# Paired values, fp4 multiplications of three chunks on GpSimd and new due times in a planned two-layer kernel

## The chip, the cores and the metric

The kernel runs on one core of one Trainium2 chip. The metric is the device time of one execution in microseconds (us). The core has five engines that run their own instruction streams: TensorE (PE, with its weight loads as PEld), VectorE (DVE), ScalarE (ACT), GpSimd (POOL) and SyncE (SP), which here issues every DMA. All of the kernel's data are float32 at the interface.

## The reference

The input is `x` of shape [8, 1024, 256]: 8 sequences of 1024 rows. Four residual steps follow one another, each on a layernorm of `x` without gain:

```
x = x + L0_attn(layernorm(x))   # decoder layer with causal "flow" attention, 16 heads of 16, wo, layernorm,
                                # gelu FFN 256 -> 1024 -> 256, layernorm
x = x + L0_ffn(layernorm(x))    # relu(n @ w1 + b1) @ w2 + b2, width 1024
x = x + L1_attn(layernorm(x))   # softmax attention over 1024 rows, one head of 256
x = x + L1_ffn(layernorm(x))    # fp4(silu(fp4(n) @ fp4(wg).T) * (fp4(n) @ fp4(wu).T)) @ fp4(wd).T, width 704
```

The second attention is what the change's first part touches:

```
Q, K, V = split(t @ W_qkv.T + b_qkv);  softmax(Q @ K.T / sqrt(256)) @ V
```

`fp4` takes blocks of 16 neighbours of a row, scales each by its largest magnitude over 6, rounds to the grid 0, 0.5, 1, 1.5, 2, 3, 4, 6 and scales back. It is applied to the weights and to both inputs of the last FFN's matmuls, so that the gated product `hid` (128 rows by 704) of every chunk passes through it.

## The kernel before

**Tiling.** The 8192 rows are 64 chunks of 128 (`P`). Four chunks (`G`) make a group, 16 groups in all, two to a sequence, eight chunks (`NCH`) to a sequence. Matmuls take 128 by 128 weights and stream 128 to 512 columns into one of eight PSUM banks. The first layer runs group by group: flow attention on 32-row tiles of TensorE (the rows of the profile with `kz`), the two dense FFNs as two loops over eight blocks of the width (`w_in` into `hidden`, `hidden` into `w_out`), then `norms_1` and `norms_2`. The dense weights don't stay in SBUF: `load_weights` streams them for each group, 256 KB a load, into two buffers of `w_in` and two of `w_out`, so that a load can start only when the matmuls on the buffer's last content are done. The second layer runs chunk by chunk in `soft_chunk`, once all eight chunks of a sequence have been normed: scores against both groups of keys, exponentials, transposed probabilities times the values `vt`, then fp4 of the normed rows, gate and up, `hid`, fp4 of `hid`, down, and the output.

**norms_2** ends the first layer for a chunk: layernorm `n`, the turn of `n` into `n2T` (256 features on partitions, rows in the free dimension; it serves as key, query input and value input), and then two matmuls with `wv3` for the chunk's values, and one DVE addition of the bias row `bsv` into `vt`. `q["normed"]` counts the chunks of a sequence that are through.

**fp4** on a `hid` of 128x704: a maximum per block of 16 (`x_amax`), the scale `x_s` and its reciprocal `x_r` (128x44 each), a multiplication by the reciprocal and a constant (`hid<-hid,x_r`), a square on ACT into `q_c`, two DVE steps that round by adding and subtracting, and a multiplication by the scale (`hid<-hid,x_s`). The turn of `hid` into `hqT` follows.

**flip** turns a 128x256 block in one of two ways. The far way is a copy on POOL into `cut` (as 16-bit halves), a DMA transpose on SP's queue into `spun` and a copy on ACT. The near way is two transposes on PE into a bank and a copy on ACT. The near way is taken where the planner finds that PE is short of ready work (`plan.idle`).

**The order** of all instructions on every engine is made when the program is built. Each part of the work is a generator that yields what its next instruction needs; `Plan` holds a clock for each engine, costs every instruction in `took`, and always advances the part that could start with the least wait for PE, ties going to the part with the earliest due time `at`. The engines then run exactly in that order: each instruction has a dependence on the one before it on its engine. Due times and waits come from the table `T`, overridden by the entries of `EARLY`, each of which holds until a time on the planner's PE clock (130, 260, 400, 2150 and the end). Where the planner expects PE to stand still for over 1.6 us, `fill` puts dummy multiplications of the identity by itself there (`bank<-ident` in the profile). `Queue.issue` records every instruction, so that all rows of the profile carry its line, L431, and are told apart by tile names: `mx` is the row maximum of the scores, `prob` the exponentials, `ln_ve` and `ln_rstd` the two steps of a layernorm on POOL, `res` and `xr` residual rows with a bias added on POOL.

Of the kernel before, what the change touches and what calls it, by code (L numbers as in the profile page):

```python
# [14 lines left out]
ALU = mybir.AluOpType  # L15
AX = mybir.AxisListType

P = 128
D = 256
# [4 lines left out]
INTER = 704  # L24
# [7 lines left out]
    span=-0.073, prods=0.129, pair=0.137, sums=0.037, weighted=0.239, sums2=0.231, chunk=0.625,  # L32
# [5 lines left out]
    gate1=1, gate2=1, by_act=1,  # L38
)
LAG = 2  # L40
QB = 16
G = 4
GT = G * P
# [41 lines left out]
        gate2=3.5,  # L85
# [6 lines left out]
        gate1=3.5, prods=0.091, weights=0.002,  # L92
    )),
    (400.0, dict(
        prods=-0.044, pair=0.237, weighted=0.037, chunk=0.696, turn_k=0.968, xo=0.327,
        turn_h=0.707, step=0.103, norm=0.746, soft=3.784, soft1=0.31, soft3=0.912, fp4=2.195,
        weights=0.078, ripe_d=7.107, ahead=0.839, lin2=-0.414, dense1=-0.101, norm1=0.415,
    )),
    (2150.0, dict(
        span=-0.281, prods=-0.047, pair=0.211, sums=0.062, weighted=0.312, scores=0.625,  # L100
        turn_k=0.801, xo=0.501, turn_h=0.706, soft3=1.013, fp4=3.733, fp4_over=6.383,
        ripe_g=0.463, ripe_d=6.945, back=1.258, ahead=1.548, lin1=0.497, lin2=-0.186,
        lin3=-0.398, dense0=0.006, dense1=-0.298, norm0=-0.113, norm1=-0.214, weights0=-0.286,
        gate1=3, shy=0.438, gate2=4, lin0=0.25,
    )),
    (1000000000.0, dict(
        lin3=0.54, ripe_d=5.647, lin1=0.423, dense1=-0.149, scores=0.713, ripe_g=0.601, xo=0.287,
        chunk=0.609, shy=1.216, back=0.633, sums2=0.358, ripe_t=0.0, soft2=0.39, ahead=1.438,
        step=0.155, span=-0.165, weights=0.092, ripe_s=0.0, fp4=3.709, turn_k=0.743,
        weighted=0.307, norm=0.386, fp4_over=3.982, sums=-0.024, gate1=2, prods=0.13, gate2=3.5,  # L110
        norm1=0.603, lin0=0.38,
    )),
]

# [18 lines left out]
class Plan:  # L133
# [96 lines left out]
    def took(self, queue, op, args, kw):  # L230

        aps = [x for x in list(args) + list(kw.values()) if isinstance(x, bass.AP)]
        outs = [kw["out"] if "out" in kw else aps[0]]
        if kw.get("accum_out") is not None:
            outs.append(kw["accum_out"])
        size = 1
        for ap in aps:
            n = 1
            for d in ap.shape[1:]:
                n *= d  # L240
            size = max(size, n)

        overlap, after = 0.0, 0.035
        if queue == "tensor":
            size = 1
            for d in outs[0].shape[1:]:
                size *= d
            cost = size * (0.853e-3 if op == "transpose" else 1.687e-3)
            tiled = op == "matmul" and (kw["lhsT"].shape[-1] <= 32 or kw["lhsT"].shape[0] <= 32)
            if tiled or op == "matmul" and kw["lhsT"].dtype == BF16:  # L250
                cost *= 0.25
            if tiled != self.tiled:
                cost += 0.2
            self.tiled = tiled
            after = 0.2
        elif queue == "vector":
            each = {"reciprocal": 6.2e-3, "tensor_tensor_scan": 2.15e-3}.get(op, 1.05e-3)
            cost = 0.17 + each * size
            if op == "tensor_scalar" and outs[0].dtype == BF16:
                cost = 0.16 + 0.26e-3 * size  # L260
            elif op == "scalar_tensor_tensor" and any(ap.shape[-1] == 1 for ap in aps):
                cost += 0.06
            if size >= 256 and not any(ap.tensor.name in self.banks for ap in aps):
                cost *= 1.12
            overlap = 0.08
        elif queue == "scalar":
            cost = (0.16 if op == "copy" and outs[0].dtype != U16 else 0.26) + 0.82e-3 * size
            for x in args:
                if not isinstance(x, bass.AP) and self.SETS.get(x, self.act_set) != self.act_set:
                    self.act_set = self.SETS[x]  # L270
                    self.free[queue] = self.free.get(queue, 0.0) + 1.3
            if kw.get("accum_out") is not None:
                cost += 0.15
            overlap = 0.1
        elif queue == "gpsimd":
            cost = 0.65 + 0.7e-3 * size
            if op in ("tensor_scalar", "iota"):
                cost = 0.22
            elif op == "memset":
                cost = 0.1 + 0.9e-3 * size  # L280
            elif op == "tensor_copy":
                cost = 0.2 + 1.0e-3 * size
        else:
            wide = op != "dma_start_transpose" and size > 256
            cost = 1.34 if op == "dma_start_transpose" else 0.6 if wide else 0.54
        start = self.free.get(queue, 0.0)
        if queue not in ("tensor", "sync"):
            start = max([start] + [self.used.get(ap.tensor.name, 0.0) for ap in outs])
        for ap in aps:
            name = ap.tensor.name  # L290
            if self.by.get(name) != queue or queue in ("vector", "gpsimd"):
                start = max(start, self.done.get(name, 0.0) + (0.05 if queue == "gpsimd" else 0.0))
            if name not in self.done and name in self.held:
                start = max(start, self.used[name])
        if queue == "tensor":
            if start - self.ran > 2.0:
                self.slow = start + 2.1
            if start < self.slow:
                cost *= 2
            self.ran = start + cost  # L300
        if queue == "sync":
            start = max(start, self.landed.pop(0))
        end = start + cost
        if queue == "sync":
            n = 2e-6 / 180e-3 if op == "dma_start_transpose" else 4e-6 / 320e-3
            for d in outs[0].shape:
                n *= d
            self.free["rings"] = max(self.free.get("rings", 0.0), end) + n
            after = self.free["rings"] - end + (0.75 if op == "dma_start_transpose" else 1.8)
            self.landed.append(end + after)  # L310
        self.free[queue] = end - overlap
        for ap in outs:
            self.done[ap.tensor.name] = end + after
            self.by[ap.tensor.name] = queue
        for ap in aps:
            name = ap.tensor.name
            self.used[name] = max(self.used.get(name, 0.0), end + after)
            if queue != "tensor" and name not in self.kept:
                self.held.discard(name)
# [17 lines left out]
    def pe(self, *tiles, **kw):  # L337
        return self.need("tensor", tiles, **kw)
# [111 lines left out]
def block_stack_kernel(ctx: ExitStack, tc: tile.TileContext, a: dict, out: bass.AP):  # L450
# [346 lines left out]
    def two(t):  # L797
        return t.rearrange("p (k t) -> p k t", k=2)

    def blocks(t, width):  # L800
        return t[:, :width].rearrange("p (b e) -> p b e", e=QB)

    def wide(v, rows, nb):
        return v.unsqueeze(2).to_broadcast([rows, nb, QB])

    def fp4(src, width, rows=P, factor=1.0):

# [13 lines left out]
        rc = small([P, INTER // QB], "x_r", 2)[:rows, :nb]  # L823
        nc.vector.reciprocal(rc, sc)
        yield dve(rc)
        nc.vector.scalar_tensor_tensor(
            blocks(src, width),
            blocks(src, width),
            -factor * (1.0 - 2.0**-23),
            wide(rc, rows, nb),  # L830
            ALU.mult,
            ALU.mult,
        )
        tile_c = yield from fresh("q_c", act(src))
        c = tile_c[:rows, :width]
        nc.scalar.activation(c, src, AF.Square, scale=(2.0**22 / 6.0) ** 0.5)
# [3 lines left out]
        yield dve(src)  # L840
        nc.vector.scalar_tensor_tensor(src, c, k, src, ALU.add, ALU.subtract)
        plan.drop(tile_c)
        nc.vector.tensor_tensor(
            blocks(src, width), blocks(src, width), wide(sc, rows, nb), ALU.mult
        )

# [156 lines left out]
    def running(out, cur, carry, b, first, last):  # L1003
# [14 lines left out]
    flows = B * NG  # L1018
    seqs = [{"past": {"chunks": 0}, "n2T": {}, "vt": {}, "normed": 0} for _ in range(B)]
    groups = [  # L1020
        {"res": {}, "hT": {}, "nT": {}, "turned": {}, "scaled": set(), "ran": set(), "away": {}}
        for _ in range(flows)
    ]
    count = {
# [669 lines left out]
    def norms_2(p, i, acc, taken):  # L1694
# [14 lines left out]
        if g not in q["n2T"]:  # L1709
            q["n2T"][g] = two(kept([P, 2 * GT], "n2T", 4))  # L1710
        n2 = q["n2T"][g]
        here = slice(i * P, (i + 1) * P)
        yield from flip(two(n), n2[:, :, here], last=n)
        yield pe(
            n2,
            banks=1,
            when=lambda: "values" in late
            and (s < 2 or count["valued"] >= (s - 1) * NCH)
            and (p == 0 or count["attended"] >= 3 * G),
        )  # L1720
        if g not in q["vt"]:
            q["vt"][g] = kept([P, G, D], "vt", 4)
        bank = mm_bank()
        for k in range(2):
            nc.tensor.matmul(
                bank[:, :D], lhsT=n2[:, k, here], rhs=wv3[:, k, :], start=k == 0, stop=k == 1
            )
        yield dve(bank)
        nc.vector.tensor_tensor(q["vt"][g][:, i, :], bank[:, :D], bsv, ALU.add)
        q["normed"] += 1  # L1730


    def soft_chunk(cc):
# [120 lines left out]
            nc.vector.tensor_tensor(hid[:, cols], hid[:, cols], ub, ALU.mult)  # L1854
        plan.drop(xqT)
        yield dve(hid)
        yield from fp4(hid, INTER, factor=0.5)
        hqT, pairs = [], []
        for half in range(2):
            tq = yield from fresh("prob", plan.pool(hid, at=at + times["soft3"]), "hqT")  # L1860
# [91 lines left out]
```

## Time and profile before

| what | value |
|---|---|
| runs | 2435.72, 2436.44, 2437.16 us; median 2436.44 |
| the profiled execution's own time | 2438.24 us |
| its span (first to last instruction) | 2436.5 us |
| its mean granted clock | 0.998 |
| busy: PE, DVE, ACT, POOL | 2411.5, 1899.1, 1408.5, 1255.0 us |
| last PE instruction ends at | 2433.2 us |
| DMA: share of 16 engines by SP's transfers, transposes issued | 53.0%, 771 |
| ACT table loads | 139, 1.283 us each |

In a row of a group of instructions stand line, engine, operation, output<-inputs, shapes, count, then busy time and the mean ns of one, then the engine's idle time just ahead of them with what ended it. In the timeline a row begins with its start and length in us, and a bracket tells a wait ahead of it and its releaser; `x8` counts instructions that were drawn together. A busy PE is one that has a matmul in its pipeline.

### The profile page before, as it was taken

The page shows a single profiled execution, that of the slowest core. Times are in us where ns is not written, and L with a number is a line of the kernel's source. Part 1 is how long each engine was busy: PE and PEld are TensorE (multiplying, and loading weights), DVE is VectorE, ACT ScalarE, POOL GpSimd, SP SyncE. Part 2 cuts the span into 40 slices and gives each one's busy share as a digit, 9 for nine tenths or more (in the row PEclk, how much of TensorE's full clock was granted, in tenths as well). Part 3 has the DMA queues.
Part 4 walks back from the last instruction along what each step waited for, and adds up shares of the span by engine and source line. Part 5 has one row for each costly group of instructions (what it writes and reads, how often), then busy time and mean ns, then how long its engine had stood idle before and what let it go on. Part 6 is the DMA issues. An engine that isn't in the chain of part 4 may idle for free.

```text
span 2436.5 us, 46855 instructions
## 1 busy us (share of the span) xinstructions
PE 2411.5 (99%) x16103; PEld 1868.0 (77%) x16103; DVE 1899.1 (78%) x4121; ACT 1408.5 (58%) x2882; POOL 1255.0 (52%) x2261
## 2 busy tenths in 40 slices
PE   8999999999999999999999999999999999999998
PEld 6787777777777777787777777787777777787766
DVE  7887776878778787787869778787877968766688
ACT  5546455465565645656565565655656665545454
POOL 4455364453655655456454655556464664534342
PEclk9999999999999999999999999999999999999999
DMA  4354665455655554556555555555555655645333
GB/s 105 106 168 140 171 139 149 117 118 130 141 130 132 136 146 116 141 132 141 135 124 136 142 132 128 127 146 118 150 128 120 158 110 138 139 112 133 67 76 70
DMA packets 633103, 313.62 MB, mean 129 GB/s; under 512 B 436000, under 2 KB 621344, under 8 KB 632864
## 3 DMA queue, kind: packets, MB, share of 16 engines
q1 hardware_dynamic: 632864, 310.62, 53.0%
q8 instruction: 128, 2.10, 0.4%
q14 instruction: 111, 0.91, 0.1%
HBM read 188.43 MB, written 20.97 MB: 86 GB/s over the span
## 4 chain that ended last, share of the span: by engine, by line
PE 91%; DVE 5%; ACT 2%; POOL 1%; DMA 1%; issue 1%; DVEq 0%; POOLq 0%; ACTq 0%; SPq 0%
PE bank L431 91%; DVE prod L431 1%; DVE hid L431 1%; ACT L431 1%; POOL ln_rstd L431 0%; DVE u L431 0%; DVE ln_st L431 0%; DVE x_amax L431 0%; DMA w_in<-in_L_attn_W_dram 0%; DVE k L431 0%; POOL ln_ve L431 0%; POOL ln_shift L431 0%; ACT kz L431 0%; DVE q L431 0%; DVE sc L431 0%
## 5 line engine op out<-in xcount | busy, mean ns | idle before, releaser
L431 PE MATMUL bank<-half,w_in 128*128 128x256 f32 x2048 | 530.0, 382 | 2.5 <-DMA w_in<-in_L_attn_W_dram 1.4
L431 PE MATMUL bank<-w_out,hidden 128*128 128x256 f32 x2048 | 527.7, 384 | 3.6 <-DMA w_out<-in_L_attn_W_dram 2.6
L431 PEld LDWEIGHTS bank<-w_out,hidden 128*128 128x128 f32 x2048 | 380.2, 190 | 105.3 <-issue 46.1
L431 PEld LDWEIGHTS bank<-half,w_in 128*128 128x128 f32 x2048 | 384.1, 190 | 79.9 <-issue 20.0
L431 POOL TENSOR_SCALAR ln_ve<-ln_mv 128x1 f32<-128x1 f32 x384 | 99.8, 260 | 559.3 <-DVE ln_mv L431 528.5
L431 ACT ACTIVATE hidden<-bank,c_L_ffn_b 128x256 f32<-128x256 f32 x256 | 120.7, 472 | 222.9 <-PE bank L431 222.0
L431 POOL TENSOR_TENSOR ln_rstd<-ln_ve,neghalf 128x1 f32<-128x1 f32 x384 | 232.8, 606 | 32.0
L431 PE MATMUL bank<-n2T,qT 128*128 128x512 f32 x512 | 241.6, 594 | 0.0
L431 ACT ACTIVATE hidden<-bank,c_L_attn_b 128x256 f32<-128x256 f32 x256 | 119.7, 469 | 196.4 <-PE bank L431 195.1
L431 PE MATMUL bank<-vt,probT 128*128 128x256 f32 x1024 | 233.0, 381 | 0.0
L431 POOL COPY cut<-n 128x512 uint16<-128x512 uint16 x231 | 166.4, 726 | 110.5 <-DVE n L431 73.4
L431 PEld LDWEIGHTS bank<-vt,probT 128*128 128x128 f32 x1024 | 195.2, 191 | 33.2 <-issue 4.8
L431 POOL COPY cut<-prob 128x512 uint16<-128x512 uint16 x229 | 161.4, 727 | 86.4 <-ACT prob L431 57.2
L431 POOL COPY cut<-hid 128x512 uint16<-128x512 uint16 x170 | 120.2, 730 | 133.3 <-DVE rsum L431 50.5
L431 ACT ACT_TABLE_LOAD x139 | 178.3, 1283 | 6.8 <-DVE nmax L431 3.2
L431 PE MATMUL bank<-wdT,hqT 128*128 128x256 f32 x768 | 176.4, 379 | 0.1
L431 PE MATMUL bank<-wgT,xqT 128*128 128x352 f32 x512 | 172.8, 460 | 0.8 <-ACT xqT L431 0.8
L431 PE MATMUL bank<-wuT,xqT 128*128 128x352 f32 x512 | 172.4, 459 | 0.0
L431 ACT COPY probT<-spun 128x512 uint16<-128x512 uint16 x251 | 161.2, 672 | 16.0 <-DMA spun<-cut 15.4
L431 PEld LDWEIGHTS bank<-wdT,hqT 128*128 128x128 f32 x768 | 145.4, 190 | 22.9 <-issue 1.4
L431 PEld LDWEIGHTS bank<-n2T,qT 128*128 128x128 f32 x512 | 96.2, 190 | 69.5 <-issue 60.3
L431 DVE TENSOR_TENSOR sc<-bank,tri 128x384 f32<-128x384 f32 x240 | 116.7, 546 | 39.1 <-PE bank L431 39.0
(294 smaller groups left out, 4741.7 us busy)
## 6 DMA issues: line engine op xcount, KB each, us to landing
w_in<-in_L_attn_W_dram SPq DMA_DIRECT2D x128, 256.0 KB
w_out<-in_L_attn_W_dram SPq DMA_DIRECT2D x128, 256.0 KB
w_in<-in_L_ffn_w_dram SPq DMA_DIRECT2D x128, 256.0 KB
w_out<-in_L_ffn_w_dram SPq DMA_DIRECT2D x128, 256.0 KB
spread<-packed SPq DMA_DIRECT2D x90, 256.0 KB
spun<-cut SPq DMA_TRANSPOSE x771
x<-in_L_attn_inputs_dram SPq DMA_DIRECT2D x64, 128.0 KB
xr<-in_L_attn_inputs_dram SPq DMA_DIRECT2D x64, 128.0 KB
```

The costliest lines, as they stand in the source:

```text
L431: ins = method(*args, **kw)
```

## The change

Three things. In `norms_2` the values of chunks 2j and 2j+1 of a group are made together when both are turned: four matmuls into the halves of one bank, and one DVE addition of 128x512 with the bias row broadcast. In `fp4` of `hid`, for chunks 59, 60 and 61 (`POOLED`), the multiplication by the reciprocal and that by the scale go to GpSimd; the constant is then multiplied into the 128x44 reciprocal on DVE first. The planner costs such a GpSimd instruction at 1.5 us. And three of the five entries of `EARLY` have new values: those until 400, until 2150 and to the end.

```diff
@@ -38,6 +38,7 @@
     gate1=1, gate2=1, by_act=1,
 )
 LAG = 2
+POOLED = (59, 62)
 QB = 16
 G = 4
 GT = G * P
@@ -92,23 +93,24 @@
         gate1=3.5, prods=0.091, weights=0.002,
     )),
     (400.0, dict(
-        prods=-0.044, pair=0.237, weighted=0.037, chunk=0.696, turn_k=0.968, xo=0.327,
-        turn_h=0.707, step=0.103, norm=0.746, soft=3.784, soft1=0.31, soft3=0.912, fp4=2.195,
-        weights=0.078, ripe_d=7.107, ahead=0.839, lin2=-0.414, dense1=-0.101, norm1=0.415,
+        prods=-0.044, pair=0.237, weighted=0.037, chunk=0.696, turn_k=0.968, xo=0.316,
+        turn_h=0.707, step=0.103, dense=-0.082, norm=0.746, soft=3.784, soft1=0.31, soft3=0.912,
+        fp4=2.195, weights=0.264, shy=0.202, ripe_t=1.123, ripe_d=7.107, ahead=0.839,
+        lin2=-0.414, dense1=-0.101, norm1=0.415, soft2=0.206,
     )),
     (2150.0, dict(
-        span=-0.281, prods=-0.047, pair=0.211, sums=0.062, weighted=0.312, scores=0.625,
-        turn_k=0.801, xo=0.501, turn_h=0.706, soft3=1.013, fp4=3.733, fp4_over=6.383,
-        ripe_g=0.463, ripe_d=6.945, back=1.258, ahead=1.548, lin1=0.497, lin2=-0.186,
-        lin3=-0.398, dense0=0.006, dense1=-0.298, norm0=-0.113, norm1=-0.214, weights0=-0.286,
-        gate1=3, shy=0.438, gate2=4, lin0=0.25,
+        span=-0.205, prods=-0.047, pair=0.211, sums=0.062, weighted=0.312, turn_k=0.801,
+        xo=0.501, turn_h=0.706, soft3=1.013, fp4=3.733, fp4_over=7.303, ripe_g=0.463,
+        ripe_d=6.945, back=1.258, ahead=1.548, lin1=0.397, lin2=-0.186, lin3=-0.398,
+        dense0=0.006, dense1=-0.8, norm0=-0.113, norm1=-0.214, weights0=-0.286, weights1=-0.074,
+        gate1=3, shy=0.438, gate2=4, lin0=0.25, weights=0.303,
     )),
     (1000000000.0, dict(
-        lin3=0.54, ripe_d=5.647, lin1=0.423, dense1=-0.149, scores=0.713, ripe_g=0.601, xo=0.287,
-        chunk=0.609, shy=1.216, back=0.633, sums2=0.358, ripe_t=0.0, soft2=0.39, ahead=1.438,
-        step=0.155, span=-0.165, weights=0.092, ripe_s=0.0, fp4=3.709, turn_k=0.743,
-        weighted=0.307, norm=0.386, fp4_over=3.982, sums=-0.024, gate1=2, prods=0.13, gate2=3.5,
-        norm1=0.603, lin0=0.38,
+        ripe_d=4.893, lin1=0.423, dense1=0.15, scores=0.713, ripe_g=0.601, xo=0.287, chunk=0.609,
+        shy=1.216, back=0.503, sums2=0.358, ripe_t=0.0, soft2=0.39, ahead=1.438, step=0.155,
+        span=-0.165, weights=0.053, ripe_s=0.0, fp4=3.709, turn_k=0.743, weighted=0.307,
+        norm=0.387, fp4_over=3.982, sums=0.005, gate1=2, prods=0.13, gate2=3.5, norm1=0.328,
+        lin0=0.38, soft1=0.406, pair=0.17, ripe_v=0.561, weights0=-0.456, lin=0.147,
     )),
 ]
 
@@ -280,6 +282,8 @@
                 cost = 0.1 + 0.9e-3 * size
             elif op == "tensor_copy":
                 cost = 0.2 + 1.0e-3 * size
+            elif size > 512:
+                cost = 1.5
         else:
             wide = op != "dma_start_transpose" and size > 256
             cost = 1.34 if op == "dma_start_transpose" else 0.6 if wide else 0.54
@@ -803,7 +807,7 @@
     def wide(v, rows, nb):
         return v.unsqueeze(2).to_broadcast([rows, nb, QB])
 
-    def fp4(src, width, rows=P, factor=1.0):
+    def fp4(src, width, rows=P, factor=1.0, pooled=False):
 
@@ -823,14 +827,21 @@
         rc = small([P, INTER // QB], "x_r", 2)[:rows, :nb]
         nc.vector.reciprocal(rc, sc)
         yield dve(rc)
-        nc.vector.scalar_tensor_tensor(
-            blocks(src, width),
-            blocks(src, width),
-            -factor * (1.0 - 2.0**-23),
-            wide(rc, rows, nb),
-            ALU.mult,
-            ALU.mult,
-        )
+        if pooled:
+            nc.vector.tensor_scalar(rc, rc, -factor * (1.0 - 2.0**-23), None, ALU.mult)
+            yield plan.pool(rc)
+            nc.gpsimd.tensor_tensor(
+                blocks(src, width), blocks(src, width), wide(rc, rows, nb), ALU.mult
+            )
+        else:
+            nc.vector.scalar_tensor_tensor(
+                blocks(src, width),
+                blocks(src, width),
+                -factor * (1.0 - 2.0**-23),
+                wide(rc, rows, nb),
+                ALU.mult,
+                ALU.mult,
+            )
         tile_c = yield from fresh("q_c", act(src))
         c = tile_c[:rows, :width]
         nc.scalar.activation(c, src, AF.Square, scale=(2.0**22 / 6.0) ** 0.5)
@@ -840,7 +851,9 @@
         yield dve(src)
         nc.vector.scalar_tensor_tensor(src, c, k, src, ALU.add, ALU.subtract)
         plan.drop(tile_c)
-        nc.vector.tensor_tensor(
+        if pooled:
+            yield plan.pool(src)
+        (nc.gpsimd if pooled else nc.vector).tensor_tensor(
             blocks(src, width), blocks(src, width), wide(sc, rows, nb), ALU.mult
         )
 
@@ -1018,7 +1031,7 @@
     flows = B * NG
     seqs = [{"past": {"chunks": 0}, "n2T": {}, "vt": {}, "normed": 0} for _ in range(B)]
     groups = [
-        {"res": {}, "hT": {}, "nT": {}, "turned": {}, "scaled": set(), "ran": set(), "away": {}}
+        {"res": {}, "hT": {}, "nT": {}, "turned": {}, "scaled": set(), "ran": set(), "away": {}, "there": set()}
         for _ in range(flows)
     ]
     count = {
@@ -1711,23 +1724,38 @@
         n2 = q["n2T"][g]
         here = slice(i * P, (i + 1) * P)
         yield from flip(two(n), n2[:, :, here], last=n)
+        there = groups[p]["there"]
+        there.add(i)
+        if i % 2 == 0:
+            return
         yield pe(
             n2,
             banks=1,
-            when=lambda: "values" in late
+            when=lambda: i - 1 in there
+            and "values" in late
             and (s < 2 or count["valued"] >= (s - 1) * NCH)
             and (p == 0 or count["attended"] >= 3 * G),
         )
         if g not in q["vt"]:
             q["vt"][g] = kept([P, G, D], "vt", 4)
         bank = mm_bank()
-        for k in range(2):
-            nc.tensor.matmul(
-                bank[:, :D], lhsT=n2[:, k, here], rhs=wv3[:, k, :], start=k == 0, stop=k == 1
-            )
+        for j in range(2):
+            for k in range(2):
+                nc.tensor.matmul(
+                    bank[:, j * D : (j + 1) * D],
+                    lhsT=n2[:, k, (i - 1 + j) * P : (i + j) * P],
+                    rhs=wv3[:, k, :],
+                    start=k == 0,
+                    stop=k == 1,
+                )
         yield dve(bank)
-        nc.vector.tensor_tensor(q["vt"][g][:, i, :], bank[:, :D], bsv, ALU.add)
-        q["normed"] += 1
+        nc.vector.tensor_tensor(
+            q["vt"][g][:, i - 1 : i + 1, :],
+            bank.rearrange("p (j d) -> p j d", d=D),
+            bsv.unsqueeze(1).to_broadcast([P, 2, D]),
+            ALU.add,
+        )
+        q["normed"] += 2
 
     def soft_chunk(cc):
@@ -1854,7 +1882,7 @@
             nc.vector.tensor_tensor(hid[:, cols], hid[:, cols], ub, ALU.mult)
         plan.drop(xqT)
         yield dve(hid)
-        yield from fp4(hid, INTER, factor=0.5)
+        yield from fp4(hid, INTER, factor=0.5, pooled=POOLED[0] <= cc < POOLED[1])
         hqT, pairs = [], []
         for half in range(2):
             tq = yield from fresh("prob", plan.pool(hid, at=at + times["soft3"]), "hqT")
```

## The prediction

> **What bounds the kernel now.** First the page: span, busy shares, chain.
>
> ```profile
> span 2436.5 us, 46855 instructions
> ...
> PE 2411.5 (99%) x16103; PEld 1868.0 (77%) x16103; DVE 1899.1 (78%) x4121; ACT 1408.5 (58%) x2882; POOL 1255.0 (52%) x2261
> ...
> PE 91%; DVE 5%; ACT 2%; POOL 1%; DMA 1%; issue 1%; DVEq 0%; POOLq 0%; ACTq 0%; SPq 0%
> ```
>
> TensorE is busy for 2411.5 of 2436.5 us, so at most 25.0 us of waits can be won without taking matmuls away. Next, stretches of 60 us tell where they lie (columns: stretch; us, busy PE, PEld, DVE, ACT, POOL with counts; granted clock, DMA share, GB/s).
>
> ```profile
> 240.00:300.00 60.00, 57.44 (x465) 47.75 (x464) 49.80 (x116) 27.25 (x67) 23.88 (x47) 1.00 0.62 168
> 360.00:420.00 60.00, 57.80 (x310) 44.90 (x308) 37.63 (x85) 38.29 (x75) 28.41 (x51) 1.00 0.62 149
> 420.00:480.00 60.00, 59.59 (x365) 45.92 (x366) 49.57 (x105) 28.98 (x64) 23.32 (x42) 0.97 0.50 126
> 480.00:540.00 60.00, 58.71 (x461) 45.23 (x460) 40.47 (x100) 37.14 (x75) 37.91 (x74) 0.97 0.50 115
> 1740.00:1800.00 60.00, 60.00 (x307) 47.03 (x307) 50.16 (x104) 30.48 (x64) 29.16 (x52) 1.00 0.60 144
> ```
>
> Between 540 and 2340 us the stretches look like the last one: nothing to win. The waits are before 540 and in the tail, and two stretches also show a clock of 0.97, which is 60 x 0.03 = 1.8 us each. The timeline shows the two waits ahead of these dips.
>
> ```profile
> 414.55 1.97 SPq L431 DMA_TRANSPOSE spun<-cut  x1
> 416.61 0.54 SPq L431 DMA_DIRECT2D w_out<-in_L_attn_W_dram  x1
> 417.26 1.78 SPq L431 DMA_TRANSPOSE spun<-cut  x1
> 420.41 3.36 PE L431 MATMUL bank<-w_out,hidden 128*128 128x256 f32 x8 [2.62 <-DMA w_out<-in_L_attn_W_dram]
> ...
> 503.51 1.34 PE L431 MATMUL bank<-q,kz 32*128 32x128 f32 x32 [1.29 <-ACT kz L431]
> ```
>
> The load of w_out stood in SP's queue behind a transpose, was issued at 416.61 and used at 420.41, 3.80 us later. Its buffer had come free only 8 matmuls (3.46 us of PE work) before its next use. Two loads of w_in cost 1.03 us at 268.89 and 0.34 at 256.10 in the same way. Then the tail:
>
> ```profile
> 2376.67 1.17 POOL L431 COPY cut<-prob 128x512 uint16<-128x512 uint16 x2 [2.59 <-ACT prob L431]
> 2377.25 1.33 DVE L431 SCALAR_TENSOR_TENSOR hid<-hid,x_r 128x704 f32<-128x704 f32 x1
> ...
> 2418.01 2.62 PE L431 MATMUL bank<-ident 128*128 128x128 f32 x22
> ...
> 2424.77 0.87 PE L431 MATMUL bank<-ident,k 128*128 128x128 f32 x6 [1.55 <-DVE k L431]
> ...
> 2429.41 0.88 PE L431 MATMUL bank<-ident,hid 128*128 128x128 f32 x6 [0.89 <-DVE hid L431]
> ```
>
> Tail waits: 2.62 (eleven dummy multiplications, so 0.24 each) + 1.55 + 0.89 + 0.75 + 0.20 (at 2399.71 and 2405.14) = 6.0 us, all behind DVE's fp4 work. Prices, by groups with shapes apart (busy us, mean ns):
>
> ```profile
> L431 DVE TENSOR_TENSOR vt<-bank,b_L_attn_b_v 128x256 f32<-128x256 f32 x64 | 26.0, 413 | 23.8 <-PE bank L431 23.7
> L431 DVE TENSOR_REDUCE mx<-bank 128x1 f32<-128x512 f32 x128 | 86.8, 678 | 41.1 <-PE bank L431 40.7
> L431 DVE TENSOR_TENSOR hid<-hid,x_s 128x704 f32<-128x704 f32 x58 | 59.3, 1023 | 2.0
> L431 DVE SCALAR_TENSOR_TENSOR hid<-hid,x_r 128x704 f32<-128x704 f32 x58 | 54.7, 943 | 0.3
> L431 POOL TENSOR_TENSOR xr<-xr,b_L_attn_ln_b 128x256 f32<-128x256 f32 x64 | 49.5, 786 | 0.1
> L431 POOL TENSOR_TENSOR res<-res,b_L_ffn_b 128x256 f32<-128x256 f32 x64 | 57.2, 895 | 10.3 <-ACT n L431 9.6 <-ACT carry_w L431 0.2
> L431 POOL TENSOR_SCALAR ln_ve<-ln_mv 128x1 f32<-128x1 f32 x384 | 99.8, 260 | 559.3 <-DVE ln_mv L431 528.5 <-DVE rsum L431 16.5
> ```
>
> **Values for two chunks.** 64 DVE adds of 0.413 us become 32; no row has an add of 128x512, the reduction of that size takes 0.678: 32 x 0.678 - 26.4 = -4.7 us of DVE. PE issues the same matmuls. DVE is 78% busy and PE waits for none of this in mid run, so I take 0. PE's order is fixed, so a late odd chunk holds all that stands behind its four matmuls. Cover: the even chunk's values wait for the odd chunk, but the softmax of a sequence needs all eight chunks. If that cover is gone, the last pair of a sequence comes later by the longer add, 0.27 us, times 8 = 2.1; the other end is -4.7 x 5% (DVE's share of the chain) = -0.2.
>
> **Due times.** These move the order on every engine. The first 794 PE instructions (some 170 us) are unchanged, so about 10 us of early waits stay. From the two orders:
> - Weight loads. The PE work between a buffer's release and its next use is 3.46 us three times around 400 us before; after, its least there is 4.95, above the 3.80 that the late load took, and at the 268.89 wait it goes from 7.36 to 7.8 or more. Four releases of 4.32 us before 255 us cost nothing in this run. Gone: 2.62 + 1.03 + 0.34, and the dip of 1.8 behind the first: -5.8. If one such wait forms again: -3.2.
> - The wait for kz (1.29) and the dip behind it (1.8): ten kz groups now follow attention groups directly, other work lies ahead of them: -3.1; or 0 if ACT is late again.
> - Dummy multiplications: eleven in the tail become four, and ten stand in three runs elsewhere (two before 250 us of PE work, one near 2043). Ten x 0.24 = 2.4, plus what was left to wait behind such runs before (0.77, 0.56, else nothing; mean 0.2) three times: +3.0. Ends: 2.4, and 2.4 + 3 x 0.77 = 4.7.
> - PE transposes instead of DMA transposes: h 18 to 24, hid 10 to 18, n 50 to 46, flow and vt 6 to 0: +4 at about 0.2 us: +0.8. Eight fewer switches to and from 32-row tiles, about 0.1 each by the pitch of matmuls beside them: -0.8. Together 0, ends -0.9 and +0.8. SP issues two transposes fewer.
>
> **fp4 on GpSimd, chunks 59 to 61.** DVE loses 3 x (0.943 + 1.023) and gains three scales of 128x44, near 0.2: -5.3 us. No row has a 128x704 multiplication on POOL. From 0.786 + 0.895 over two = 0.84 for 256 columns and 0.26 for one: 0.26 + (0.58 / 256) x 704 = 1.85 us. Ends: 0.26 + (0.526 / 256) x 704 = 1.71, and 0.895 x 2.75 = 2.46. I take 1.85, the line through the nearest rows.
>
> [...]
>
> What hangs on it: the first POOL multiplication lies between the reciprocal and ACT's square, the second before the transposes, whose cuts are POOL's own. Behind them on POOL stand other chunks' cuts and layernorm steps, each up to 1.85 late, but POOL is busy for only 3.50 us after 2400. A chunk's chain grows by 0.2 + 1.85 - 0.94 + 1.85 - 1.02 = 1.9 plus handovers, 2.0; three chunks 6.0, of which interleaved chunks cover half: +3.0. A DVE instruction beside a POOL one is slower: hid by x_s takes 0.892 us free of POOL (26 of them) and 1.129 beside it (32); the 1.33 at 2377.25 lies over the cut. Six POOL operations x 0.22 = +1.3. Against this, DVE has 53.3 us of work behind the last chunk's row maximum and PE 53.0 before; after, 55.6 and 59.6: 4.3 us of the 6.0 go. Net 0. Ends: relief alone with half the chain, -3.5 (with 0.7 of blocking escaped), and the dear operation, 6 x 0.61 = 3.7 and more on the chain: +4.
>
> [...]
>
> **Sum.** -5.8 - 3.1 + 3.0 + 0 + 0 + 0 = -5.9. The profiled execution took 2438.24 us, 1.8 above the median of the runs, 2436.44. Against the median: 2430.5 us. With the favourable ends, -5.8 - 3.1 + 2.4 - 0.9 - 3.5 - 0.2 = -11.1 (2425); with the dear ones, -3.2 + 4.7 + 0.8 + 4 + 2.1 = +8.4 (2445).
>
> **Rivals.** *A, slower:* a wait that recurs in each group of mid run. PE transposes for hid and h are chosen where the planner sees TensorE short of work; between 480 and 2060 us they fall at 13 places instead of 9, one in each 145 us, and a dummy run stands at 2043. If each of 11 groups costs what kz's wait cost, 1.29, the sum is 14.2 - 5.9 = +8.3: 2445. It eats the gain at 0.54 us a group and decides for slower from 0.98. Against it: such places cost nothing before (60.00 of 60.00). *B, no change:* the late load or the wait for kz comes again one place later with its dip (2.62 + 1.8 + 1.29 = 5.7): 2436; or the POOL operation is dear and the tail gives +4: 2434.5. For it: a queue of SP with 771 transposes, and no margin known for kz. *That the change does not do what it says:* chunks 62 and 63, the last to finish, keep DVE; then the tail's 6.0 us stay and only the chain's growth counts, within B's bounds.
>
> **Chances.** A difference of 0.2%, 4.9 us, is about what measurement tells from none. Forecast 0.50 (faster); B 0.26 (same); A 0.24 (slower). Likeliest case alone: 2425 to 2434. With A and the ends: 2423 to 2446.
>
> **What would show it.** Right: no wait for w_out or kz between 400 and 520 us, both stretches at clock 1.00, PE still 60.00 in mid run, tail waits of 5 to 7 us. Wrong: stretches of mid run below 59.5, POOL multiplications over 2.5 us, a wait for spun or hid each 145 us, or a new w_in or w_out wait over 2 us.

## The result and the profile after

The changed kernel takes 2445.44 us (median of 6 runs, 2442.77 to 2446.06) against 2436.09 us before (6 runs beside them, 2435.38 to 2437.16): a ratio of 1.0037, 95% interval 1.0026 to 1.0047. It is slower by 9 us where 6 us less were forecast, and lies at the far edge of the stated range. The profiled execution took 2445.96 us.

The page after, in the rows that the prediction shows of before:

```profile
span 2444.3 us, 46813 instructions
...
PE 2409.5 (99%) x16113; PEld 1867.4 (76%) x16113; DVE 1901.7 (78%) x4087; ACT 1400.2 (57%) x2866; POOL 1262.8 (52%) x2265
...
PE 90%; DVE 5%; ACT 2%; POOL 1%; DMA 1%; issue 1%; SPq 0%; DVEq 0%; POOLq 0%; ACTq 0%
```

TensorE is busy for 2 us less in a span 7.8 us longer, so waits grew by some 10 us. The stretches tell where (the columns as in the prediction):

```profile
180.00:240.00 60.00, 55.47 (x452) 43.74 (x450) 41.95 (x96) 39.50 (x78) 30.84 (x57) 1.00 0.53 141
240.00:300.00 60.00, 51.10 (x427) 40.91 (x424) 43.10 (x94) 24.16 (x57) 21.26 (x40) 0.94 0.47 133
360.00:420.00 60.00, 59.78 (x369) 45.49 (x370) 39.62 (x86) 36.29 (x72) 25.24 (x48) 1.00 0.63 145
420.00:480.00 60.00, 60.00 (x345) 47.29 (x347) 49.30 (x110) 34.84 (x75) 34.09 (x63) 1.00 0.59 141
480.00:540.00 60.00, 59.79 (x529) 47.18 (x519) 49.38 (x110) 36.50 (x74) 33.83 (x67) 1.00 0.49 112
```

The three lower rows are the gain that was forecast: no wait at 420 or 503 us, clock at 1.00. The second row is the loss: 8.90 us of waits and a clock of 0.94; the first has 4.53 us of waits, where before has 1.36:

```profile
180.00:240.00 60.00, 58.64 (x462) 46.03 (x461) 46.53 (x104) 40.98 (x83) 34.51 (x60) 1.00 0.49 140
```

As waits (length less busy PE) and lost clock (length times what the granted clock lacks of 1), from stretches cut at the same times in both traces, in us:

| stretch | before | after |
|---|---|---|
| 168 to 258 | 2.9 | 5.7 |
| 258 to 300 | 1.0 | 7.7, and 3.4 of clock (0.92) |
| 300 to 420 | 2.2 | 0.8 |
| 420 to 540 | 1.7, and 3.6 of clock (0.97) | 0.2 |
| 540 to 2280 | 0.1 | 1.3 |
| sum | 11.5 | 19.1 |

The difference, 7.6, is close to that of the spans, 7.8. The half clock behind the longest wait lasts from 273.5 to 280.3 us and begins inside the wait, so some 0.7 us of the 19.1 is counted twice. The tail is level (6.8 and 6.9 us of waits behind 2280), and so is the start: 1.8 us more of waits up to 168, against a half clock from 30.7 to 34.1 us that before's profile has and after's has not. Here is the place in the timeline of the changed kernel, and behind it the two waits that before has for such loads up to 300 us:

```profile
258.54 0.50 SPq L435 DMA_DIRECT2D rows<-res  x1
...
262.01 0.33 SPq L435 DMA_DIRECT2D res<-away  x1
...
264.32 0.38 SPq L435 DMA_DIRECT2D w_in<-in_L_ffn_w_dram  x1
...
264.80 2.50 SPq L435 DMA_TRANSPOSE spun<-cut  x2
...
267.17 1.10 PE L435 MATMUL bank<-half,w_in 128*128 128x256 f32 x4 [1.98 <-DMA w_in<-in_L_ffn_w_dram]
...
267.40 2.52 SPq L435 DMA_DIRECT2D spread<-packed  x4
...
269.83 0.83 PE L435 MATMUL bank<-ident 128*128 128x128 f32 x6
...
270.01 0.54 SPq L435 DMA_DIRECT2D w_out<-in_L_ffn_w_dram  x1
...
274.97 2.08 PE L435 MATMUL bank<-w_out,hidden 128*128 128x256 f32 x4 [4.30 <-DMA w_out<-in_L_ffn_w_dram]
...
276.83 1.91 PE L435 MATMUL bank<-half,w_in 128*128 128x256 f32 x4
...
278.54 1.91 PE L435 MATMUL bank<-wo,xo 128*128 128x256 f32 x4
```

```profile
256.10 1.10 PE L431 MATMUL bank<-half,w_in 128*128 128x256 f32 x4 [0.34 <-DMA w_in<-in_L_ffn_w_dram]
...
268.89 1.13 PE L431 MATMUL bank<-half,w_in 128*128 128x256 f32 x4 [1.03 <-DMA w_in<-in_L_attn_W_dram]
```

SP's issues came in the order of the program here. The load of w_out stands behind two transposes (2.50) and four transfers of 256 KB (2.52), leaves at 270.01 and is used 4.96 us later. Ahead of it SP had stood from 259.0 to 262.0: `res<-away` writes a buffer whose own store, `rows<-res`, had to be done first. The four matmuls at 274.97 take 2.08 us, the next two groups of four 1.91 each, where 1.03 is usual: TensorE's granted clock is 0.50 from 273.5 to 280.3 us.

All of this lies ahead of the first effect of the new due times: run e8, with all of before's due times, has the same order on every engine up to there and the same two waits (2.85 and 3.55 us). The order between 168 and 270 us is what the planner makes of paired values under due times that were left as they were.

### The profile page after: what moved, and what is told of

Same layout as the page of the kernel before. It is cut to its first block, busy times and chain, and to the rows that moved or that the text cites. A ratio compares the mean times of both kernels' runs of the same rounds, so it can differ in the third digit from the quotient of the medians.

```text
span 2444.3 us, 46813 instructions
## 1 busy us (share of the span) xinstructions
PE 2409.5 (99%) x16113; PEld 1867.4 (76%) x16113; DVE 1901.7 (78%) x4087; ACT 1400.2 (57%) x2866; POOL 1262.8 (52%) x2265
## 3 DMA queue, kind: packets, MB, share of 16 engines
q8 instruction: 127, 2.08, 0.4%
## 4 chain that ended last, share of the span: by engine, by line
PE 90%; DVE 5%; ACT 2%; POOL 1%; DMA 1%; issue 1%; SPq 0%; DVEq 0%; POOLq 0%; ACTq 0%
PE bank L435 90%; DVE prod L435 1%; ACT L435 1%; DMA spun<-cut 1%; DVE hid L435 0%; DVE n L435 0%; DVE sc L435 0%; DMA w_out<-in_L_ffn_w_dram 0%; POOL ln_rstd L435 0%; DVE u L435 0%; DVE ln_st L435 0%; DMA w_in<-in_L_ffn_w_dram 0%; DVE x_amax L435 0%; DVE k L435 0%; POOL ln_shift L435 0%
```

## Experiments

Ratios are against runs of the kernel before that were made beside each run (median 2435.87 to 2436.84 us), with 95% intervals. The changed kernel's is 1.0037 [1.0026, 1.0047].

**e1: one load ahead of four transfers, in the changed kernel's order.** Issues on SP are named by their count: those in `HELD` are held back until the one at `AHEAD`, the load of w_out, is out. The planner is told the old order.

```diff
+    HELD, AHEAD = range(184, 188), 188
...
+            if self.name == "sync" and n in self.HELD:
+                self.held.append(lambda: real(args, kw))
+                self.plan.took(self.name, op, args, kw)
+                return None
...
+            if self.name == "sync" and n == self.AHEAD:
+                for late in self.held:
+                    late()
```

> The changed kernel with one step moved: on SP's queue one load of w_out is issued ahead of four spread transfers of 256 KB instead of behind them (near 270 us); all else keeps its order. Theory 1 (the order that pairing gives to SP's queue starves the dense matmuls there, 4.30 us of wait at 274.97, and TensorE's clock falls behind it, 3.6 us in the stretch 240 to 300): the load leaves 2.5 us earlier and lands alone, the wait falls below 1 us, the dip is gone, and the time is 6 to 8 us less than the changed kernel's 2445.4: 2437.5 to 2439.5. Rival (the wait only stands for work that is short anyway: DVE and the groups behind would be late in its place): the wait turns up within the next 30 us, total within 2 us of 2445.4.

Measured: 2443.58 us, ratio 1.0027 [1.0017, 1.0037]. The intervals overlap, so the times alone do not tell it from the changed kernel. In the traces, from the group of matmuls at 250.21 (255.94 here, after a slower start of this execution) to the one at 360.05 (360.87) it takes 104.9 us instead of 109.8; e4 and e10, which have the changed kernel's order there, take 109.8 and 107.3. The wait of 4.30 is gone, the stretch 258 to 300 has a clock of 1.00. The wait for w_in ahead of it stays (2.51), as the move does not touch it, and smaller waits of 0.65 and 0.61 follow. SP's order at this one place is worth 2.4 to 4.9 us by the traces: theory 1, short of its 6 to 8 by what came next.

**e7: the same, and `res<-away` behind the next load of w_in.** `MOVES` gives, for a count on SP, the issues that are held back until it is out.

```diff
+    MOVES = {181: [178], 188: [184, 185, 186, 187]}
```

> The changed kernel with two moves on SP's queue: the load of w_out ahead of the four spread transfers as in e1, and the load of res that waits for its buffer's own store (SP stood from 259.0 to 262.0) put behind the next load of w_in, so that w_in no longer queues behind that wait. Theory (SP's order is what costs between 258 and 275 us): the wait of 1.98 to 2.5 us for w_in near 267 us goes as well, 6 to 8 us below the changed kernel: 2437.5 to 2440. Rival (w_in's buffer or the DMA engines bound it, not SP's order): as e1, 4 to 5 us below, with a wait for w_in of over 1.5 us left.

Measured: 2440.45 us, 1.0013 [1.0004, 1.0023], clear of the changed kernel's by about 0.24%, and 0.45 us short of the forecast 2437.5 to 2440. Its timeline at the same place:

```profile
262.30 0.38 SPq L435 DMA_DIRECT2D w_in<-in_L_ffn_w_dram  x1
...
265.88 0.53 SPq L435 DMA_DIRECT2D w_out<-in_L_ffn_w_dram  x1
...
266.47 2.52 SPq L435 DMA_DIRECT2D spread<-packed  x4
...
269.44 1.13 PE L435 MATMUL bank<-w_out,hidden 128*128 128x256 f32 x4 [0.41 <-DMA w_out<-in_L_ffn_w_dram]
```

The load leaves at 265.88 and is used 3.56 us later with 0.41 of wait; the w_in ahead of it is not waited for, the granted clock is 1.00 from 258 to 300 us, and the next w_in, at 275.87, is waited for by 0.99 us. From the group at 250.21 (250.63) to that at 360.05 (353.63) it takes 103.0 us, 6.8 less than in the changed kernel and 4.3 less than in e10. Two positions in one queue make up most of the loss of the second stretch; 168 to 258 keeps its 6.1 us of waits.

**e2: pairing from group 4 on, third entry as before.** `single = p < 4` keeps the old code for the first four groups.

```diff
+        single = p < 4
+        if i % 2 == 0 and not single:
+            return
```

> The changed kernel, but groups 0 to 3 make their values chunk by chunk as before, and the entry of due times until 400 is the one of before; then the order is that of before for the first 400 us. Theory 1 (the loss lies between 168 and 300 us, where pairing reorders the work under due times that were not changed): waits there as before (about 4 us instead of 17), later parts as in the changed kernel; 2429 to 2434. Rival (pairing or the new due times cost in mid run, or GpSimd costs in the tail): 2442 or more.

Measured: 2437.31 us, 1.0002 [0.9992, 1.0012]: level, where theory 1 expected 2429 to 2434. The early waits are those of before, as it said, so the loss is gone; but the waits near 420 (1.66) and, in a new place, 513.70 (1.57) are there, and so the gain is gone too.

**e13: pairing from group 1 on, third entry as before.** As e2 with `p < 1`: four chunks of 64 unpaired.

> The changed kernel with only group 0 unpaired (its four chunks' values one by one), and the entry of due times until 400 as before. The order is that of before for the first 260 us. If the loss is that of the first group's pairs under unchanged due times: waits of 4 to 5 us between 168 and 300 instead of 17, and 2430 to 2435, faster than both kernels. Rival (wherever pairing starts, the order it makes has late loads or transfers soon behind): new waits of 5 us or more between 260 and 540, and 2436 to 2442.

Measured: 2432.51 us, 0.9987 [0.9978, 0.9996]: 4.2 us faster than before beside it, and the fastest of all by the ratios. Its stretches:

```profile
180.00:240.00 60.00, 58.80 (x461) 45.98 (x461) 46.32 (x104) 41.09 (x83) 34.56 (x61) 1.00 0.49 139
240.00:300.00 60.00, 58.07 (x464) 48.02 (x463) 49.56 (x113) 28.81 (x69) 25.41 (x49) 1.00 0.61 167
420.00:480.00 60.00, 59.42 (x375) 45.72 (x374) 54.59 (x115) 32.69 (x72) 31.29 (x57) 1.00 0.52 134
```

3.1 us of waits between 180 and 300 instead of 13.4, and nothing of the kind behind. The interval ends close to 1, so the gain over before is small. e13 differs from the changed kernel in two things, the first group and the third entry; but e8, with the old entry and all pairs, has the waits. So the loss is that of the first group's pairs, in the stretch that kept its due times, and the rest of the change, without its new third entry, is worth having.

**e9: pairing in the order of before.** The planner is told the old instructions (`ghost`: accounted, not issued); the later chunk of a pair issues four matmuls and one addition (`quiet`: issued, not accounted).

```diff
+                ghost=True,
...
+        if both:
+            for j in range(2):
+                for k in range(2):
+                    nc.tensor.matmul(
...
+                        quiet=True,
```

> The kernel before with pairing, and nothing else moved: the planner is told the old instructions, so that every engine keeps the order of before, and the four matmuls and the one addition of 128x512 stand where the later chunk of a pair had its own. Theory (pairing costs nothing by itself, the new order that the planner makes of it does): level with before within 1.5 us, waits between 168 and 300 us as before (about 4 us), DVE 4 to 5 us less busy. Rival (half a sequence's values coming later, or four matmuls in a row, hold up the work behind them): 3 us or more slower, with waits before bank<-wv3,n2T or bank<-vt,probT.

Measured: 2437.07 us, 1.0004 [0.9995, 1.0013], DVE busy 1895.7 us instead of 1899.1 (3.4 less, where 4 to 5 were expected). Pairing itself is level; what the planner made of it cost.

**e8 and e3: pairing and GpSimd with all of before's due times; the new due times alone.** Only the table `EARLY` is exchanged.

> The changed kernel with all of before's due times: pairing and GpSimd's multiplications alone. Its order is the changed kernel's up to 268 us. Theory (pairing itself costs where it reorders work under due times set for another order, and the new entries win part of it back): the same waits of 17 us or so between 168 and 300, and slower than the changed kernel, 2450 to 2470. Rival (the pairing is harmless and the new due times are what costs): 2436 or less.

> The kernel before with the three new entries of due times alone: no pairing, no multiplication on GpSimd. The order is that of before for the first 340 us. Theory 1: no loss before 300 us, so nothing near 2445 from there; what the new entries give to an order they were not set for is open: 2433 to 2443. Rival (the new due times are themselves the loss): 2445 or more, with waits between 300 and 2340 us.

Measured: e8 2473.71 us, 1.0146 [1.0129, 1.0163]; e3 2455.85 us, 1.0074 [1.0059, 1.0089]. e8 has the changed kernel's early waits (2.85 and 3.55 for the two loads), 8.1 us of waits between 540 and 2280, and TensorE busy for 2425.4 us, with 254 records of dummy multiplications instead of 180; it is slower than the 2450 to 2470 expected. e3 missed theory 1's 2433 to 2443 and lies where its rival said, 2445 or more: no loss before 300 us, but 5.9 us of waits between 540 and 2280, and 58 records of dummy multiplications in the tail, where before has 22. The rival does not explain the changed kernel, which waits 1.3 us between 540 and 2280. Each table fits one order: the change without its new table costs 37 us, the table alone 19, both together 9. Neither part's effect can be added up from the other's.

**e4 and e10: the multiplications back on DVE, with the tail planned anew, and in the kept order.**

```diff
-POOLED = (59, 62)
+POOLED = (0, 0)                                          # e4
...
-            nc.gpsimd.tensor_tensor(                       # e10
...
+            for engine, how in ((nc.gpsimd, "ghost"), (nc.vector, "quiet")):
+                engine.tensor_tensor(
```

> The changed kernel with the fp4 multiplications of chunks 59 to 61 back on DVE; its order differs from the changed kernel's only after 2380 us. The prediction's term (net 0 in the tail, -3.5 to +4): 2445.4 within 2. [...]

> The changed kernel with the order on every engine kept, but the six fp4 multiplications of 128x704 issued to DVE in the place where GpSimd had them. e4, where the planner made the tail anew for DVE, was 5.4 us slower than the changed kernel. If GpSimd itself gains (DVE is what the tail waits for): 4 to 7 us above the changed kernel's 2445.4, so 2449 to 2452. If the gain in e4 is the planner's new order: within 2 us of 2445.4.

Measured: e4 2450.85 us, 1.0056 [1.0041, 1.0071]; e10 2448.48 us, 1.0049 [1.0034, 1.0065]. e4 is 4.6 us slower than the changed kernel by the ratios, past the 2 us that went with the prediction's term; the intervals just overlap, but each of its runs (2448.49 us or more) is slower than each of the changed kernel's (2446.06 or less). Its tail is planned anew, so this is GpSimd and order together. e10, which keeps the order, fell between its two expectations: 2.9 us, intervals overlapping. So a gain from GpSimd in the new order is likely, but its size is not settled. In e10's trace the waits behind 2395 us are 4.95 us instead of the changed kernel's 2.78, most of the difference at `bank<-ident,k` (1.85 against 0.51).

**e11 and e14: GpSimd alone on the kernel before, three chunks and six.**

```diff
+POOLED = (59, 62)    # e11; (56, 62) in e14
```

> The kernel before with the GpSimd multiplications of chunks 59 to 61 alone (old due times, no pairing); the order is that of before up to the last 60 us. By the traces the six cost 1.41 us each, not 1.85: the chain of three chunks grows by 3.3 us, half of it covered, and 5.3 us leave DVE, on which the tail waits 6.0 us: 2 to 4 us less than before. The prediction's own term: within 2 us of before. Rival (only the new last entry of due times makes use of it): level or slower.

> As e11 (the kernel before, GpSimd multiplications alone), but for six chunks, 56 to 61, instead of three. If DVE's load in the tail is the bound: another 0.5 to 2 us below e11's 2435.1. Rival (GpSimd's longer chain and its own queue of cuts take over): 2436 or more.

Measured: e11 2435.08 us, 0.9996 [0.9987, 1.0005]; e14 2437.54 us, 1.0009 [1.0000, 1.0019]. Both have the tail planned anew under the old due times. Three chunks gain nothing that can be told from none, below the 2 to 4 us expected and within the prediction's own term. Six give no further gain; the time is where the rival put it, with 1.49 us of wait for `k` and 0.94 for `hid` in the last 20 us, but the interval begins at 1.0000, so a loss is not clear.

**e5: the prediction's term by itself: before, with the load at 416.61 ahead of the transpose.**

```diff
+    MOVES = {311: [310]}
```

> The kernel before with one step moved on SP's queue: the load of w_out that TensorE waited 2.62 us for at 420.41 is issued ahead of the transpose that began at 414.55, not behind it. This is the prediction's term for that wait by itself (2.62 + 1.8 of clock). Theory: the wait falls to 0.2 to 0.6, the stretch 420 to 480 shows a clock of 1.00, and the time is 3 to 4.4 us below before. Rival (the transpose or a later load is late in its place): a new wait of 1 us or more before 450 us, and less than 2 us gained.

Measured: 2435.57 us, 0.9996 [0.9987, 1.0005]. In its timeline:

```profile
418.41 1.10 PE L431 MATMUL bank<-w_out,hidden 128*128 128x256 f32 x4 [0.33 <-DMA w_out<-in_L_attn_W_dram]
...
420.66 1.13 PE L431 MATMUL bank<-w_out,hidden 128*128 128x256 f32 x4 [1.15 <-ACT hidden L431]
```

The load's wait falls from 2.62 to 0.33 and the granted clock stays at 1.00 from 420 to 480 us, but the very next group now waits 1.15 us for ACT's `hidden`, which had been hidden behind it. From 409.0 (409.29) to the group at 426.20 (424.22) the trace is 2.3 us shorter, not 4.4, and the medians differ by 0.9 us, which can't be told from none: the rival, in its new wait and in its small gain.

**e6 and e12: combinations.** e6 is e2 with e5's move; e12 is e9 with e5's move and e11's multiplications.

> Pairing from group 4 on, due times of before until 400 and the new ones behind, GpSimd's multiplications, and the same one load moved ahead of its transpose near 415 us. Run e2, without the move, was level with before (2437.3 against 2436.8) and waited 1.66 us there. If the gains add, 3 us below e2: 2434, and 2 to 3 us faster than before. Rival: the work behind the load is short too (1.57 us at 513.70 stays in any case), and it stays level with before within 1.5 us.

> The kernel before with pairing in the old order (as e9), the one load of w_out ahead of its transpose near 415 us (as e5, which was 0.9 us below before and cut the trace there by 2.3), and the GpSimd multiplications (as e11). If the three add: 2431 to 2435, faster than both kernels. Rival (run e11 or e9 loses what e5 wins): 2436 or more.

Measured: e6 2435.97 us, 0.9999 [0.9990, 1.0008]; e12 2435.51 us, 1.0002 [0.9993, 1.0011]. Neither adds up to what can be told from no change, so no sum of the small gains is shown.

## Why the prediction was wrong

**Weight loads: the step that failed.** It read a load's margin from TensorE's work between a buffer's release and its next use, 7.8 us or more near 269, against 3.80 for a late load, and booked -5.8. But here a load left only when SP reached it. In the changed kernel SP reached one 2.4 us and the next 4.5 us later than in e7 (counted from the same group of matmuls), behind `res<-away`, two transposes and four transfers, in that very place. The term came out as follows: the wait at 420 and its dip went (-4.4 by the trace of before), the waits of 0.34 and 1.03 became 1.98 and 4.30 with 3.4 of clock (+8.3): +3.9 for -5.8, or about +3.5 without what waits and dips have in common. e7 shows that the queue's order does it, and it is no chance of one execution: e4, e8 and e10, with the same order there, wait 6.6, 6.4 and 4.9 us for the two loads, where the changed kernel waits 6.3. The order of SP's instructions was at hand for both kernels; the term used TensorE's alone.

**Dummy multiplications.** Priced at 0.24 each and 0.2 of wait behind a run. The second run (the three at 269.83) stands just ahead of the 4.30. A dummy run marks a place where the planner expects TensorE to stand still; what stands behind it is that place's own wait, 4.30 us here and 0.41 behind the same run in e7, and not the mean of runs in another order.

**A stretch without a term.** The order was said to be unchanged up to 170 us, and no wait was booked for the 90 us behind, but for what dummy runs leave. They cost 2.8 us more, mostly in small waits for ACT, such as these:

```profile
183.82 1.10 PE L435 MATMUL bank<-w_out,hidden 128*128 128x256 f32 x4 [0.76 <-ACT hidden L435]
...
194.24 1.13 PE L435 MATMUL bank<-w_out,hidden 128*128 128x256 f32 x4 [1.11 <-ACT hidden L435]
...
216.52 1.98 PE L435 MATMUL bank<-n0T,wk 128*128 128x512 f32 x4 [1.39 <-ACT q L435]
```

Which step of pairing is behind each is open; e2 and e13, which leave the first group unpaired, don't have them.

**The price of the wait at 420.** It came from one execution. The same order up to there shows waits of 1.56 to 1.93 us in e2, e9, e11 and e14, and a clock of 1.00 in both stretches: the 2.62 and the two dips were the dear end. The transpose ahead of the load kept SP for 1.97 us in before's profile and for 1.23 in e2's. And e5 shows another 1.15 us to be ACT's. From these, 1 to 2 us is an estimate of a fair price, not 4.4.

**kz.** Right: the wait (1.28 to 1.31 in each run with before's order there) is gone. Its dip comes and goes: a clock of 0.97 from 480 to 540 us in e5 as before, 1.00 in e9, e11 and e14.

**Values.** Right as a cost: pairing in the old order is level (e9), the addition takes 0.678 us as taken from the row of `mx`. Wrong as an edit: it was taken to move nothing, and it moved the order of everything behind it.

**GpSimd.** Net 0 in the tail came out nearly as a sum, with waits of 6.8 and 6.9 us behind 2280 (counted as the prediction did, with the dummy multiplications, its 6.0 became some 4.5), but by luck: its parts were wrong and made up for each other. The multiplications took 1.38 to 1.48 us but for one, not 1.85: the line had been laid through an instruction of another kind with one column, 0.26 us, where a line through 0.84 at 256 columns and 1.4 at 704 would give 0.5. In the new order they seem to gain some 3 to 5 us (e10, e4, neither clear of noise by its interval), and the new order of the tail is then worse by as much without them; under the old due times they gain nothing that could be measured (e11). The prediction's rows of `hid<-hid,x_s` (0.892 us free of POOL, 1.129 beside it) have their like in the trace after:

```profile
2393.39 1.48 POOL L435 TENSOR_TENSOR hid<-hid,x_r 128x704 f32<-128x704 f32 x1 [2.26 <-DVE x_r L435]
...
2393.67 1.49 DVE L435 TENSOR_TENSOR n<-n,x_s 128x256 f32<-128x256 f32 x1
...
2401.01 0.42 DVE L435 TENSOR_TENSOR n<-n,x_s 128x256 f32<-128x256 f32 x1
```

The same DVE instruction takes 1.49 us beside GpSimd's multiplication and 0.42 beside none. Only three of DVE's instructions met it clearly (1.07, 0.37 and 0.42 us lost), and one GpSimd multiplication took 2.10 instead of 1.39: 2.6 us in all, twice the 1.3 booked.

**Rivals.** A, a wait in each group of mid run, forecast +8.3 and so nearly hit the time, but by luck: between 540 and 2280 the changed kernel waits 1.3 us in all. B's mechanism, a late load again in another place, is what happened, at twice its price and with the old wait gone. Among the signs of being wrong that the prediction named, a new wait for w_out of over 2 us came true.

**Of the whole:** with four of 64 chunks left unpaired and the third entry as before the change gives 2432.5 us (e13), close to the 2430.5 forecast. That does not prove the later steps one by one, as two of their prices were wrong; it does show that the one stretch turned a small gain into a loss.

## What to carry to other kernels

When an order is planned by machine, an edit's own cost says little: compare, for each transfer that the bound engine waits for, what stands ahead of it in its queue before and after, instruction by instruction from the first difference on, and give every stretch with a new order a term and a risk. Due times tuned for one order are part of that order; where a change starts to act ahead of the entries that were set anew, let it start later. Take the price of a wait from several executions, and look at what is late next to it before booking all of it.

## What the runs showed of the hardware

- After the wait of 4.30 us the matmuls ran at half speed (groups of four at 2.08, 1.91 and 1.91 us for 1.03; a granted clock of 0.50 from 273.5 to 280.3 us, and of 1.00 from 270 to 273.5 and from 280.3 to 300); three dummy multiplications stood just ahead of the wait. Before's 2.62 also came with a dip (0.97 over 60 us), and waits of 1.6 to 1.9 in the same place with none in e9 and e11 (1.00). The length of the one wait does not decide it here: the wait of 1.3 for kz came with a dip in before and e5 (0.97 from 480 to 540) and with none in e9, e11 and e14 (1.00), and one of 2.51 near 273 us in e1 with none (1.00 from 258 to 300). Why is open.
- A load of 256 KB was used 3.56 us after its issue when it went ahead of four others (e7) and 4.96 us after it when it went behind them; TensorE stood waiting for it in both, for 0.41 and 4.30 us.
- The DVE instruction `n<-n,x_s` took 1.49 us beside a GpSimd multiplication of 1.48 and 0.42 beside none; `q<-q,bank` kept its 0.52 beside a GpSimd multiplication of 1.39 (at 2410.79 and 2410.35 us in the trace after).
